# A graph attention kernel of two layers: prologue work regrouped and moved into the steps, one-hot products added in pairs

## Chip, cores and metric

The kernel runs on one core of one Trainium2 chip. The metric is the device time of one execution in microseconds (us). A core has a matrix engine (PE, with its weight loads shown as PEld), a vector engine (DVE), a scalar engine (ACT), a general engine (POOL) that also issues the indirect gathers, and a sync engine (SP) that issues plain transfers.

## The reference

A graph has N = 6250 nodes with 256 features and E = 200,000 edges with 32 attributes, sorted by destination. Rows of x are normalised and rectified, pass two graph attention layers (four heads of 64, then one of 256), and x is added at the end. Cut to what matters:

```python
def _gat(x, src, dst, ea, Wg, a_s, a_d, Wge, a_e, b, n, h, f):
    hx = (x @ Wg).reshape(n, h, f)
    he = (ea @ Wge).reshape(-1, h, f)
    al = leaky_relu(einsum(hx, a_s)[src] + einsum(hx, a_d)[dst] + einsum(he, a_e), 0.2)
    m = segment_max(al, dst)
    al = exp(al - m[dst]);  al = al / segment_sum(al, dst)[dst]
    out = segment_sum(hx[src] * al[:, :, None], dst)
    return out.reshape(n, h * f) + b

# te: edge attributes of a layer; a self loop with the mean of a node's te is added per node
te = relu(edge_attr @ We + be) * exp(x @ Wo + bo)[src][:, None]
h  = relu(layernorm(x))
x  = x + (_gat1(relu(_gat0(h) + h)) + relu(_gat0(h) + h) + h)
```

## The kernel before

**Tiles and steps.** The sorted edges are laid out as 128 partitions x 24 columns, a *step*. There are NS = 66 steps a layer (64 of 24 columns, then one of 14 and one of 13), numbered k = 0 to 131 over both layers. A table T of node rows (features after the weights, attention terms, an exponential) lies in memory for each layer; 24 indirect gathers of POOL (`gather`, L874) fetch the 128 source rows of each column into one of three buffers G.

**A step**, in the order in which its engines take the work: gathers of the next step; `logits` and `ends` (attention logits and two scans per edge row, with `pen`, a mask that is a large negative number where a destination begins); `spread` and `parts` of the next step (one-hots of destination blocks from `lb`, and parts of the node rows `tw`, which SP loads in `nodes`); `rphase1` of the next step (edge attributes times weights on PE, L958, rectified into R on ACT, L963); `links` (scans over 128 edge rows, L1096); `maxima`; `rphase2` and `adst` (into a PSUM tile `zad`, L972, L1032); `scale` (G times the weights, L1171); `sums` (one-hot products of G on PE, L1183), whose end frees G for the gathers of a later step; `edge_rows` (a transpose of zad, L1046); `onehots` (L1003); then the rows of the step before are finished and stored. `index_on` ends the step: seven turns of a generator that prepares the index masks of the next group of four steps (`index_group`). The order on each engine is the program's; waits are put in by the framework from tiles read and written.

**The prologue** (L201 to L401) makes T of layer 0. It loads x in 49 tiles (nine groups of two to seven) and gathers x for the 24 columns of step 0 (`first_rows`, L250; 8 gathers ahead of the loop, then one a tile from tile 4). These 24 columns are further tiles in G0, four groups of six. `stats` gives each group's mean and inverse root (DVE; for groups 3 to 8 a chain of small operations on POOL, L282 to L299); then each tile is normalised (ACT, L310), transposed (PE, L316; ACT, L318), multiplied (PE, L431) and kept with its bias (DVE, L435). A finished group is stored to T. `step(g)` hands out the turns of `stats` up to group g. Between the tiles DVE also takes the turns of `indices`, among them the checks of the index ranges (some 13 operations on one partition), and from the last tiles on those of `later`: folds of attention vectors into layer 0's edge weights and layer 1's weights (`fold`, `fold_e`, L170 to L195).

**Start of the steps.** `edges` (L616) zeroes five tiles `tws` on DVE (L633), loads and prepares step 0 and enters the loop.

**The layer boundary.** `ending` runs steps 64 and 65, whose node rows the first steps of layer 1 need, and prepares step 66, the first of layer 1. Step 66 gathers rows before the last 128 node rows are final, so `add_last` (L843) builds one-hots O from row numbers and adds 24 products with those 128 rows (`last`) into G, 260 columns wide:

```python
y = self.ps_y.tile([P, 1024], F32, name="y")
for i in range(c):
    h = y[:, 512 * (i % 2):512 * (i % 2) + L.TW]
    nc.tensor.matmul(h, st["O"][:, i, :], st["last"], start=True, stop=True)
    V.tensor_add(G[:, i, 0:L.TW], G[:, i, 0:L.TW], h)
```

`ps_y` and `ps_1` hold one buffer of each tile name (y, and zad, u).

Of the kernel before, what the change touches and what calls it, by code (L numbers as in the profile page):

```python
# [31 lines left out]
P = 128  # L32
# [47 lines left out]
class Kernel:  # L80
# [32 lines left out]
    def consts(self, wp):  # L113
# [3 lines left out]
        make_identity(nc, self.ident)  # L117
        self.wg, row, wpk = [], [], []
        self.ones = cp.tile([P, 1], F32, name="ones")
        nc.gpsimd.memset(self.ones, 1.0)  # L120
        self.bias, self.webd, self.be, wge = [], [], [], []
        for L in self.L:
            q = (nc.scalar, nc.sync)[L.l]
            wg = cp.tile([P, 2, L.MW], F32, name=f"wg{L.l}")
            q.dma_start(wg, a[f"wg{L.l}"].rearrange("(k p) m -> p k m", p=P))
            r = wp.tile([P, 3, D], F32, name=f"row{L.l}", bufs=1)
            q.dma_start(r.rearrange("p k d -> p (k d)"), a[f"row{L.l}"][0:3 * D].partition_broadcast(P))
            if L.l == 0:
                nc.scalar.activation(wp.tile([P, 1], F32, name="tab", bufs=1), self.ones, AF.Exp)
            self.wg.append(wg)  # L130
            row.append(r)
            b = cp.tile([P, L.MW], F32, name=f"bias{L.l}")
            nc.sync.dma_start(b, a[f"row{L.l}"][3 * D:].partition_broadcast(P))
            w = cp.tile([P, P + 1], F32, name=f"webd{L.l}")
            nc.sync.dma_start(w, a[f"we{L.l}"][:, 0:P + 1])
            e = wp.tile([P, D], F32, name=f"wge{L.l}", bufs=1)
            nc.sync.dma_start(e, a[f"we{L.l}"][:, P + 1:])
            self.bias.append(b)
            self.webd.append(w[:, 0:P])
            self.be.append(w[:, P:P + 1])  # L140
            wge.append(e)
# [29 lines left out]
        def fold(L):  # L171

            H = L.H
            for k in range(2):
                for j, c0 in ((0, L.p), (1, L.ad)):
                    t = wp.tile([P, D], F32, name="wtmp", bufs=4)
                    V.tensor_mul(t, self.wg[L.l][:, k, 0:D], row[L.l][:, j, :])
                    yield
                    V.tensor_reduce(self.wg[L.l][:, k, c0:c0 + H], t.rearrange("p (h f) -> p h f", h=H),
                                    axis=AX.X, op=OP.add)  # L180
                    yield

        def fold_e(L):

            H = L.H
            wea, we1 = self.wea[L.l]
            t = wp.tile([P, D], F32, name="wtmp", bufs=4)
            V.tensor_mul(t, wge[L.l], row[L.l][:, 2, :])
            yield
            V.tensor_reduce(we1, t.rearrange("p (h f) -> p h f", h=H), axis=AX.X, op=OP.add)  # L190
            yield
            for j in range(2):
                r = slice(j * PH, (j + 1) * PH)
                V.tensor_copy(wea[r, 32 * j:32 * j + H], we1[r, :])
            yield  # L195

        def later():
            yield from fold_e(self.L[0])
            yield from fold(self.L[1])
            yield from fold_e(self.L[1])  # L200

        return fold(self.L[0]), later()

    def prologue(self):
# [7 lines left out]
        with ExitStack() as c:  # L212
# [21 lines left out]
            warm = pt.tile([P, 2, P], F32, name="pT")  # L234
            for i in range(28):
                nc.tensor.matmul(warm[:, i % 2, :], self.ident, self.ident, start=True, stop=True)
# [18 lines left out]
            rows0 = first_rows()  # L255
            for _ in range(8):
                next(rows0, None)

            def stats(g):

                n, x = len(groups[g]), xs[g]
                st = wp.tile([P, GT, 6], F32, name="st", bufs=2)
                mv = wp.tile([P, GT, 2], F32, name="mv", bufs=3)
                s = wp.tile([P, 3, GT], F32, name="sc", bufs=3)
                for i in range(n):
# [35 lines left out]

            for i in range(0, CX, 6):
                xs[len(groups)] = G0[:, i:min(i + 6, CX), 0:D]
                groups.append(list(range(NT + i, NT + min(i + 6, CX))))
            tiles = [(g, i, t) for g, ts in enumerate(groups) for i, t in enumerate(ts)]
# [38 lines left out]
            def step(g):  # L344

                for q in list(ahead):
                    if q > g:
                        return
# [8 lines left out]
            for k in range(-3, len(tiles) + 1):  # L357
# [7 lines left out]
                if n0 is not None:  # L365
                    w = min(P, N + P - n0)
                    nc.sync.dma_start(self.T[1][n0:n0 + w, :], zero[:w, :2 * self.L[1].TW])
                    nc.sync.dma_start(self.part[n0:n0 + w, :], zero[:w, :self.L[1].TW])
                if 0 <= k + 1 < len(tiles):
                    turn(*tiles[k + 1])  # L370
# [12 lines left out]
                if t >= NT:  # L383
                    step(g + 2)
                if k >= 4:
                    next(rows0, None)
# [18 lines left out]
    def fixed_rows(self):  # L405
# [18 lines left out]
        for i in range(2):  # L424
            self.trow1.append(cp.tile([P, 2 * L1.TW], F32, name=f"t1row{i}"))
            nc.gpsimd.memset(self.trow1[i][:, L1.TW + D:], 0.0)

    def node_rows(self, L, hT, ps):
# [8 lines left out]
    def indices(self, wp):  # L437
# [74 lines left out]

        chk = wp.tile([1, 9, NS + 1], F32, name="chk", bufs=1)
        V.memset(chk, 0.0)
        V.tensor_scalar(chk[:, 0, :NS], ll[0:1, :], float(M - 1), None, op0=OP.is_gt)
        V.tensor_sub(qd[0:1], qlast[0:1], qbase[0:1])
        V.tensor_scalar(chk[:, 5:9, :NS], qd[0:1], 31.0, None, op0=OP.is_gt)
        nb = wp.tile([1, NS + 1], F32, name="nb", bufs=1)
        V.tensor_copy(nb[:, :NS], base[0:1, :])
# [5 lines left out]
        yield  # L525
        V.tensor_tensor(chk[:, 3, :NS], sc0[0:1, 0, :], sc0[0:1, 2, :], op=OP.is_lt)
        V.tensor_scalar(chk[:, 0, NS:], base[0:1, NS - 2:NS - 1], float(N - P), None, op0=OP.is_lt)
# [4 lines left out]
        yield  # L532
        self.before = cp.tile([P, NS], F32, name="before")
        V.tensor_copy(self.before, dpv)
        yield

    def index_tiles(self):
# [3 lines left out]
        for s in range(NS):  # L541
# [3 lines left out]
            else:  # L545
# [3 lines left out]
                                                    for n in ("loc", "fpen", "lpen", "isl"))  # L549
        self.pen = cp.tile([P, 4 * NCH + 1], BF, name="pen")  # L550
        self.bad = cp.tile([P, 1 + len(self.groups)], F32, name="bad")
# [11 lines left out]
    def index_group(self, g, pool, di):  # L563
# [23 lines left out]
        for pen, e in zip((self.fpen, self.lpen), ends):  # L587
# [5 lines left out]
            yield  # L593
        pv = self.pen[:, 4 * o:4 * (o + w)].rearrange("p (s h c) -> p s h c", h=4, c=c)
        t = pool.tile([P, 4 * C], F32, name="gt", bufs=2)
# [3 lines left out]
        yield  # L599
        V.tensor_scalar(pv[:, :, 0, :], t3, 1.0, -BIG, op0=OP.min, op1=OP.mult)  # L600
        V.memset(self.pen[:, 4 * (o + w):4 * (o + w) + 1], -BIG)
        yield
        for h in range(1, 4):
            nc.scalar.activation(pv[:, :, h, :], pv[:, :, 0, :], AF.Copy)
            yield
        t = pool.tile([P, 4 * C], F32, name="gt", bufs=2)
# [10 lines left out]
    def edges(self, ctx):  # L617
# [12 lines left out]
        self.state = {0: None, 1: None}  # L630
        self.tws = [self.np_.tile([P, self.L[0].TW + D], F32, name=f"tw{i}", bufs=1) for i in range(5)]
        for t in self.tws:
            nc.vector.memset(t, 0.0)  # L633
        self.nodes(steps[0])
# [9 lines left out]
        self.adst(steps[0])  # L644
        self.onehots(steps[0])
        self.edge_rows(steps[0])

        pv = late = None
        self.ahead, self.rest = 1, None
        for k, st in enumerate(steps):  # L650
# [45 lines left out]
            if pv:  # L696
                self.rows1(pv)
                late = pv
            self.index_on(left)
            if k + 6 == self.NS:  # L700
                self.places(steps[self.NS])
# [140 lines left out]
    def add_last(self, st):  # L842
# [4 lines left out]
                        op0=OP.subtract, op1=OP.is_equal)  # L847
        y = self.ps_y.tile([P, 1024], F32, name="y")
        for i in range(c):
            h = y[:, 512 * (i % 2):512 * (i % 2) + L.TW]  # L850
            nc.tensor.matmul(h, st["O"][:, i, :], st["last"], start=True, stop=True)
            V.tensor_add(G[:, i, 0:L.TW], G[:, i, 0:L.TW], h)

# [79 lines left out]
    def nodes(self, st):  # L933
        nc, L, s = self.nc, st["L"], st["s"]
        r = self.row(0, s)
        tw = self.tws[st["k"] % 5]
        st["tw"], st["xw"] = tw[:, :L.TW], tw[:, L.TW:L.TW + D]
# [11 lines left out]
    def rphase1(self, st):  # L949
        nc, L = self.nc, st["L"]  # L950
        l, ea = L.l, st["ea"]
        st["R"] = R = self.wp.tile([P, 2, 32 * C], F32, name="R", bufs=1)
        c = st["C"]
        for i in range(2):
# [97 lines left out]
    def logits(self, st):  # L1052
# [14 lines left out]
        yield  # L1067
        n, p0 = H * c, 4 * o
        fb, w = self.fb[st["k"] % 2], c if H > 1 else 1
        x = c - 1 + 32 * w  # L1070
        st["f"], st["b"] = f, b = fb[:, :n], fb[:, x:x + n]
        st["ends"] = fb[:, c - 1:c + (31 + H) * w:w]
        V.tensor_tensor_scan(f, self.pen[:, p0:p0 + n], al[:, :n], -BIG, op0=OP.add, op1=OP.max)
        yield
        V.tensor_tensor_scan(b[:, ::-1], self.pen[:, p0 + 1:p0 + n + 1][:, ::-1], al[:, :n][:, ::-1], -BIG,
                             op0=OP.add, op1=OP.max)
# [468 lines left out]
```

## Time and profile before

| | |
|---|---|
| runs, median (lowest to highest) | 4817.07 us (4813.92 to 4823.6) |
| profiled execution, its own time | 4800.02 us |
| its span | 4798.2 us |
| mean granted clock of PE over the span | 0.732 |
| prologue, until DVE begins with the steps | 0 to 145.9 us |
| layer 0, first gather to last burst before the boundary | 96.0 to 2437 us |
| boundary, three bursts and their waits | 2437 to 2624 us |
| layer 1, steady steps | 34.2 us each |

The profile lists groups of instructions by source line: busy time, then how long the engine was idle just before them and what released it. A line of the timeline has start, duration, engine, line, operation, output <- inputs, shape, and in brackets the idle time of that engine before it with the releaser. "issue" is idle time in which the engine waited for nothing that the profile shows; "remote" stands where the profile names no instruction of this core as releaser. How full the engines were in four stretches, from the view of windows (columns: stretch, its length, then busy time and number of instructions of PE, PEld, DVE, ACT and POOL, the granted clock, the share of the transfer engines and GB/s):

```profile
0.00:96.00 96.00, 78.48 (x382) 62.28 (x383) 69.93 (x319) 51.19 (x132) 48.42 (x145) 0.91 0.73 247
96.00:146.00 50.00, 27.44 (x114) 20.80 (x112) 21.66 (x97) 16.12 (x42) 22.90 (x24) 0.73 0.24 66
1000.00:1034.00 34.00, 25.82 (x80) 15.35 (x79) 23.25 (x53) 3.63 (x8) 22.84 (x25) 0.75 0.42 115
2537.00:2600.00 63.00, 29.64 (x48) 12.05 (x48) 10.68 (x26) 0.00 (x0) 39.17 (x41) 0.50 0.33 90
```

### The profile page before, as it was taken

Reading aid. Unit: us, or ns where it says so; the run is one execution under the profiler, and the core shown is the slowest. Engines: PE = TensorE matmul, PEld = TensorE weight load, DVE = VectorE, ACT = ScalarE, POOL = GpSimd, SP = SyncE. Lnnn points to the kernel's source line nnn. Section 1 sums busy time; section 2 is a strip of 40 time slices with the busy share of each in tenths; the row PEclk is TensorE's granted clock in tenths of the full one; section 3 lists DMA queues with packets and bytes.
Section 4 is the critical chain, followed back from the end, with each engine's and each line's share of the span. In section 5 each row is a group of like instructions: output and inputs, shape, how many; then the busy total and the mean of one; then the engine's idle time right before and its main releaser. Section 6 shows DMA issues by size and latency. Waiting matters only on the chain. (4 is left out here: it accounts for less than half of the span.)

```text
span 4798.2 us, 35104 instructions
## 1 busy us (share of the span) xinstructions
PE 3203.7 (67%) x9964; PEld 1948.6 (41%) x9964; DVE 2901.0 (60%) x6782; ACT 520.2 (11%) x1152; POOL 3011.0 (63%) x3249
## 2 busy tenths in 40 slices
PE   7556766767767766767765666666666666666666
PEld 5334444444444444444442333333333433333334
DVE  6556766666766666666664555555455556455556
ACT  4111111111111111111110000000000000000000
POOL 5446666666666666666644666666666666666664
PEclk8676777776777777777775777777767777777777
DMA  6334444444444444444433444444444444444442
GB/s 218 93 104 119 128 130 119 129 131 119 130 127 122 128 128 126 124 126 127 126 108 92 126 118 117 124 120 124 116 124 126 118 116 125 119 124 117 124 125 69
DMA packets 240006, 585.82 MB, mean 122 GB/s; under 512 B 64201, under 2 KB 96655, under 8 KB 239609
## 3 DMA queue, kind: packets, MB, share of 16 engines
q0 software_dynamic: 150144, 422.75, 33.6%
q1 hardware_dynamic: 89243, 160.09, 10.2%
q8 instruction: 80, 1.31, 0.1%
q14 instruction: 123, 1.01, 0.1%
q10 hardware_dynamic: 416, 0.67, 0.0%
HBM read 544.42 MB, written 38.94 MB: 122 GB/s over the span
## 5 line engine op out<-in xcount | busy, mean ns | idle before, releaser
L874 POOL DMA_INDIRECT G<-T,src x3078 | 2937.8, 954 | 1679.3 <-issue 889.1
L1183 PE MATMUL u<-G,S 128*128 128x270 f32 (+1 forms) x6252 | 1648.0, 417 | 737.7 <-issue 588.3
L1183 PEld LDWEIGHTS u<-G,S 128*128 128x128 f32 x6252 | 1257.7, 203 | 1066.7 <-issue 643.0
L958 PE MATMUL y<-ea,webd 64*128 64x384 f32 (+1 forms) x1056 | 709.6, 795 | 326.8 <-issue 293.1
L1171 DVE TENSOR_TENSOR G<-G,kps 128x6144 f32<-128x6144 f32 (+1 forms) x137 | 853.0, 6230 | 0.0
L1096 DVE TENSOR_TENSOR_SCAN cl<-fl,cl,lf 4x129 f32<-4x129 f32 (+1 forms) x130 | 61.1, 470 | 898.5 <-remote 598.6
L958 PEld LDWEIGHTS y<-ea,webd 64*128 64x128 f32 x1056 | 281.4, 289 | 605.0 <-issue 540.2
L972 PE MATMUL zad<-R,wea 128*64 128x384 f32 (+1 forms) x1056 | 447.3, 764 | 10.2 <-ACT R L963 7.3
L1003 DVE TENSOR_TENSOR S<-kps,loc 128x3072 f32<-128x3072 f32 x132 | 437.5, 3315 | 4.5
L963 ACT ACTIVATE R<-y,webd 128x768 f32<-128x768 f32 x260 | 233.2, 897 | 649.8 <-PE y L958 293.8
L972 PEld LDWEIGHTS zad<-R,wea 128*64 128x64 f32 x1056 | 149.8, 197 | 309.5 <-issue 246.9
L1188 ACT ACTIVATE U<-u 128x270 f32<-128x270 f32 (+1 forms) x132 | 52.0, 394 | 1852.8 <-remote 1004.5
L1046 DVE STREAM_TRANSPOSE rt<-zad 128x768 f32<-128x768 f32 (+1 forms) x130 | 124.6, 959 | 15.9 <-issue 10.7
L1018 PE MATMUL zad<-a,Q 128*128 128x12 bf16 (+1 forms) x132 | 23.9, 181 | 163.4 <-issue 99.6
L431 PE MATMUL fin<-wg,h1T 128*128 128x260 f32 x264 | 119.5, 599 | 1.5 <-ACT h1T L1278 1.5
L987 DVE TENSOR_TENSOR lb<-lb,kps 128x1536 bf16<-128x1536 bf16 (+1 forms) x68 | 113.5, 1669 | 0.0
L1086 PE MATMUL lf<-ident,fb 128*36 128x128 f32 (+1 forms) x132 | 45.8, 347 | 98.6 <-issue 69.2
L431 PE MATMUL ps<-wg,hT 128*128 128x266 f32 x292 | 88.3, 429 | 28.4 <-ACT hT L318 17.8
L1103 PE MATMUL lf<-ident,cl 36*128 36x36 f32 (+1 forms) x132 | 35.4, 269 | 95.9 <-DVE cl L1098 95.8
L1270 DVE TENSOR_TENSOR t1row<-t1row,fb 128x256 f32<-128x256 f32 x66 | 28.2, 427 | 112.5 <-remote 60.4
L1103 PEld LDWEIGHTS lf<-ident,cl 36*128 36x128 f32 (+1 forms) x132 | 25.3, 192 | 168.9 <-DVE cl L1098 148.7
L1018 PEld LDWEIGHTS <-Q 128*128 128x128 bf16 x132 | 14.3, 108 | 190.7 <-issue 108.1
(202 smaller groups left out, 2248.4 us busy)
## 6 DMA issues: line engine op xcount, KB each, us to landing
G<-T,src POOLq DMA_INDIRECT x3078
ea<-in_ea_dram SPq DMA_DIRECT2D x64, 768.0 KB
lb<-locrow SPq DMA_DIRECT2D x64, 384.0 KB
T<-t1row SPq DMA_DIRECT2D x66, 227.5 KB
tw<-T SPq DMA_DIRECT2D x66, 225.8 KB
tw<-T SPq DMA_DIRECT2D x66, 117.2 KB
tw<-in_x_dram SPq DMA_DIRECT2D x66, 112.0 KB
part<-t1row SPq DMA_DIRECT2D x64, 113.8 KB
```

What stands on the lines that cost most here:

```text
L431: self.nc.tensor.matmul(ps[:, :L.MW], hT[:, k, :], self.wg[L.l][:, k, :], start=(k == 0), stop=(k == 1))
L874: nc.gpsimd.indirect_dma_start(out=G[:, c, 0:L.TW], out_offset=None, in_=rows, in_offset=bass.IndirectOffsetOnAxis(ap=idx[:, c:c + 1], axi ...
L958: nc.tensor.matmul(y[:, o], self.webd[l][r, :], ea[r, w], start=True, stop=True)
L963: nc.scalar.activation(R[:, i, :32 * c].rearrange("p (b n) -> p b n", b=2), y.rearrange("p (b n) -> p b n", b=2)[:, :, :16 * c], AF.Relu, ...
L972: nc.tensor.matmul(st["zad"][i * PH:(i + 1) * PH, o], self.wea[l][0], R[:, i, w], start=True, stop=False)
L987: V.tensor_tensor(lb[:, :, :n], lb[:, :, :n], self.k_part.unsqueeze(2).to_broadcast([P, i, n]), op=OP.is_equal)
L1003: nc.vector.tensor_tensor(st["S"][:, c0:c1, :], self.k_iota.unsqueeze(1).to_broadcast(w), self.loc[:, o + c0:o + c1].unsqueeze(2).to_broad ...
L1046: V.transpose(rv[:, :32 * c].rearrange("p (b n) -> p b n", b=2), z.rearrange("p (b n) -> p b n", b=2)[:, :, :16 * c])
L1096: V.tensor_tensor_scan(cl[:H, :], fl[:H, :], lf[:H, 0:P + 1], init, op0=OP.add, op1=OP.max)
L1103: nc.tensor.transpose(pc, cl[:n, 0:P], self.ident[0:n, 0:n])
L1171: nc.vector.tensor_tensor(v, v, pw[:, c0:c1, :].unsqueeze(3) .to_broadcast([P, c1 - c0, H, L.F]), op=OP.mult)
L1183: nc.tensor.matmul(st["u"][:, :L.W], S[:, i, :], G[:, i, 0:L.W], start=(j == 0), stop=(j == c - 1))
```

## The change

1. **Gathers of x**: 14 instead of 8 ahead of the loop, the other ten at every third tile from tile 15 on instead of one a tile from tile 4.
2. **Statistics of step 0's columns** in groups of 6 and 18 instead of four of 6; turns for the group of 18 are handed out from tile 45 on only.
3. **tws**: four tiles instead of five, zeroed by POOL after the 14 gathers instead of by DVE at the start of `edges`; steps take them in turn modulo four.
4. **Moved out of the prologue**: layer 1's `fold` goes behind step 0's one-hots in `edges`; the checks and layer 1's `fold_e` are taken in two turns a step from k = 6 on. Their tiles move to the pool that stays.
5. **pen**: kept once per edge instead of four times (once a head); each step of layer 0 copies it fourfold on ACT at the start of `rphase1`, into one of two tiles `pen4`. `index_group` has 13 turns instead of 16.
6. **Idle products on PE**: 34 instead of 28 at the start, 8 more at tile 1 and 3 at tile 6.
7. **add_last**: products in pairs, into two PSUM tiles in turn (y and zad), and one add of two columns (128 x 520) for each pair.

```diff
-            for i in range(28):
+            def idle(n):
+                for _ in range(n):
+                    nc.tensor.matmul(self.kps[:, 384:512], self.ident, self.ident, start=True, stop=True)
+
+            for i in range(34):
                 nc.tensor.matmul(warm[:, i % 2, :], self.ident, self.ident, start=True, stop=True)
...
-            for _ in range(8):
+            for _ in range(14):
                 next(rows0, None)
+            for t in self.tws:
+                nc.gpsimd.memset(t, 0.0)
...
-            for i in range(0, CX, 6):
-                xs[len(groups)] = G0[:, i:min(i + 6, CX), 0:D]
-                groups.append(list(range(NT + i, NT + min(i + 6, CX))))
+            for i, e in ((0, min(6, CX)), (6, CX)):
+                if i < e:
+                    xs[len(groups)] = G0[:, i:e, 0:D]
+                    groups.append(list(range(NT + i, NT + e)))
...
-                    if q > g:
+                    if q > (g if k >= NT - 4 else min(g, g0)):
                         return
...
+                if k in (1, 6):
+                    idle(9 - k)
...
-                if k >= 4:
+                if k >= 14 and k % 3 == 0:
                     next(rows0, None)
...
-        def later():
-            yield from fold_e(self.L[0])
-            yield from fold(self.L[1])
-            yield from fold_e(self.L[1])
-
-        return fold(self.L[0]), later()
+        self.late, self.soon = fold_e(self.L[1]), fold(self.L[1])
+        return fold(self.L[0]), fold_e(self.L[0])
...
+        self.late = chain(self.late, self.checks(qd31, low))
...
-        self.pen = cp.tile([P, 4 * NCH + 1], BF, name="pen")
+        self.pen = cp.tile([P, NCH + 1], BF, name="pen")
+        self.nc.gpsimd.memset(self.pen[:, NCH:], -BIG)
+        self.pen4 = [cp.tile([P, 4 * C + 1], BF, name=f"pen4{i}") for i in range(2)]
...
-        V.tensor_scalar(pv[:, :, 0, :], t3, 1.0, -BIG, op0=OP.min, op1=OP.mult)
-        V.memset(self.pen[:, 4 * (o + w):4 * (o + w) + 1], -BIG)
-        yield
-        for h in range(1, 4):
-            nc.scalar.activation(pv[:, :, h, :], pv[:, :, 0, :], AF.Copy)
-            yield
+        V.tensor_scalar(self.pen[:, o:o + w], t[:, :w], 1.0, -BIG, op0=OP.min, op1=OP.mult)
+        yield
...
-        self.tws = [self.np_.tile([P, self.L[0].TW + D], F32, name=f"tw{i}", bufs=1) for i in range(5)]
-        for t in self.tws:
-            nc.vector.memset(t, 0.0)
...
         self.onehots(steps[0])
+        drain(self.soon)
         self.edge_rows(steps[0])
...
             self.index_on(left)
+            if k >= 6:
+                next(self.late, None)
+                next(self.late, None)
...
-        y = self.ps_y.tile([P, 1024], F32, name="y")
-        for i in range(c):
-            h = y[:, 512 * (i % 2):512 * (i % 2) + L.TW]
-            nc.tensor.matmul(h, st["O"][:, i, :], st["last"], start=True, stop=True)
-            V.tensor_add(G[:, i, 0:L.TW], G[:, i, 0:L.TW], h)
+        for i in range(0, c, 2):
+            y = self.ps_y.tile([P, 1024], F32, name="y") if i % 4 else self.ps_1.tile([P, 1024], F32, name="zad")
+            n = min(2, c - i)
+            h = y.rearrange("p (j w) -> p j w", j=2)[:, :n, :L.TW]
+            for j in range(n):
+                nc.tensor.matmul(h[:, j, :], st["O"][:, i + j, :], st["last"], start=True, stop=True)
+            g = G[:, i:i + n, 0:L.TW]
+            V.tensor_add(g, g, h)
...
-        tw = self.tws[st["k"] % 5]
+        tw = self.tws[st["k"] % 4]
...
-        c = st["C"]
+        c, o, H = st["C"], st["o"], L.H
+        st["pen"] = self.pen[:, o:o + c + 1]
+        if H > 1:
+            st["pen"] = pen = self.pen4[st["k"] % 2]
+            nc.scalar.activation(pen[:, :H * c].rearrange("p (h c) -> p h c", c=c),
+                                 self.pen[:, o:o + c].unsqueeze(1).to_broadcast([P, H, c]), AF.Copy)
```

## Prediction

> **What bounds the kernel now.** I read the engine totals first, then the costliest groups, the waits by releaser, and the timeline at four places: the prologue, the first steps, one steady step, the layer boundary. The page says which engine carries the steps:
>
> ```profile
> PE 3203.7 (67%) x9964; PEld 1948.6 (41%) x9964; DVE 2901.0 (60%) x6782; ACT 520.2 (11%) x1152; POOL 3011.0 (63%) x3249
> L874 POOL DMA_INDIRECT G<-T,src x3078 | 2937.8, 954 | 1679.3 <-issue 889.1
> L1188 ACT ACTIVATE U<-u 128x270 f32<-128x270 f32 (+1 forms) x132 | 52.0, 394 | 1852.8 <-remote 1004.5
> ```
>
> PE shows more busy time, but POOL sets the pace: one gather of a step is 0.95 us and the next starts 0.30 later, so 24 of them are a burst of 30 us, and the starts of the bursts lie 34.2 us apart in layer 1 and about 36 in layer 0. Between bursts POOL waits 4 to 6 us for the sums that free its buffer. The 1004.5 us that ACT waits with the releaser "remote" are one more trait: in a long part of each burst, until some 2 to 4 us after its last gather, the recorded semaphore updates of all engines land only about 0.7 us apart (110.89, 111.58, 112.28, 113.0, ... in step 1), so handing work from one engine to another is slow there. I call this a slow stretch. About 54 updates fall in a burst of layer 0 and 42 in one of layer 1. What the change can win lies where POOL isn't busy already. Those places are these:
>
> ```profile
> 46.14 0.43 DVE L435 TENSOR_TENSOR trow<-ps,bias 128x266 f32<-128x266 f32 x1 [3.10 <-PE pT L316]
> 49.60 0.60 ACT L310 ACTIVATE h<-x,ln 128x256 f32<-128x256 f32 x1 [2.20 <-POOL ln L299]
> 60.86 0.60 ACT L310 ACTIVATE h<-x,ln 128x256 f32<-128x256 f32 x1 [3.41 <-DMA part<-zero]
> 96.03 1.07 POOL L874 DMA_INDIRECT G<-T,src  x1 [18.40 <-ACT hT L318]
> 129.16 0.39 ACT L318 ACTIVATE hT<-pT 128x256 f32<-128x256 f32 x1 [13.83 <-remote]
> 146.05 0.95 POOL L874 DMA_INDIRECT G<-T,src  x1 [20.10 <-ACT G L329]
> 146.31 2.71 DVE L633 MEMSET tw<- 128x524 f32 x5 [0.38 <-issue]
> 162.65 0.98 DVE L1046 STREAM_TRANSPOSE rt<-zad 128x768 f32<-128x768 f32 x1 [7.05 <-issue]
> ```
> ```profile
> 2537.48 1.24 PE L851 MATMUL y<-last,S 128*128 128x260 f32 x2 [6.75 <-DVE S L846]
> 2538.76 0.43 DVE L852 TENSOR_TENSOR G<-G,y 128x260 f32<-128x260 f32 x1 [1.33 <-PE y L851]
> 2539.24 1.24 PE L851 MATMUL y<-last,S 128*128 128x260 f32 x2 [0.52 <-DVE G L852]
> ...
> 2575.36 0.42 DVE L852 TENSOR_TENSOR G<-G,y 128x260 f32<-128x260 f32 x1 [5.18 <-remote]
> ...
> 2599.51 0.43 DVE L852 TENSOR_TENSOR G<-G,y 128x260 f32<-128x260 f32 x1 [1.33 <-PE y L851]
> ...
> 2623.89 0.95 POOL L874 DMA_INDIRECT G<-T,src  x1 [35.52 <-PE zad L1018]
> ```
>
> The last fence matters most. For the first full step of layer 1, 24 one-hot products are added into the gathered rows. Both halves lie in one PSUM tile, so PE waits for DVE (0.52) and DVE for PE (1.33): 1.75 us a round, and 3.3 to 5.6 us for the seven rounds in a slow stretch (2563 to 2592). They end at 2599.94, the step's own chain ends 24 us later, and POOL, whose burst ended at 2588.4, has stood still for 35.52 us.
>
> **Part 1: the pairs (L846 to L852).** Removed: 12 adds of 0.43 us and all turns but those between tiles. With two tiles, PE fills one while DVE empties the other. A product costs PE 0.53 us by the warm L431 rows (1.06 for two such products) and 1.24 by the row above; 12 pairs are 13 to 30 us, against 62.5. An add of 128x520 is not in the trace; between 0.43 (this width halved) and 0.98 (128x768 transposed) I take 0.7, hidden behind the next pair. So the adds end between 2551 and 2568, before most of the slow stretch. But the next thing is POOL: its gathers go on to 2588.4 whatever PE does, and 4.3 us of a usual wait give 2592.7 as its earliest restart. The chain of 24 us after the adds now falls into the slow stretch; its six turns between PE and DVE cost up to 2.6 us each there (half of a 5.2 us round) instead of 1, so it ends between 2575 and 2602. Against 2623.89 that is a gain of 22 to 31; I take **28**, and for the range 15, if the stretch lasts longer.
>
> The windows give 0.50 as PE's granted clock from 2537 to 2600. The Trainium skill, TensorE: Matmul & The Clock Gate, section "Part 1: The HAM clock gate", says that the clock is halved until PE was active for about 3.4 us. By that rule the closer spaced pairs would soon be warm, and 12 pairs would take some 16 us, an estimate from it and the rows; by the row's 1.24 they take 30.
>
> **Part 2: gathers and statistics of the prologue.** Before, 13 gathers already run without a gap (5.67 to 22.0), though eight are issued ahead of the loop; so "fourteen first" changes little. The others ran in a bunch of six at 37.6 to 45.0 and one of five at 49.7 to 56.3, and POOL's own Newton steps (0.20 to 0.27 us each, some 15 for a group of tiles) stood behind them: hence the three waits of 3.10, 2.20 and 3.41 us. One gather at every third tile delays a chain by 1.25 us, not by 7.5. The undisturbed pace is 1.12 us a tile. Of the 8.7 us of these waits I take back 5. DVE is full from 80 to 100 us (18.96 of 20); the checks leave there (3.5 us of 78.92 to 84.7), and two groups of statistics instead of four save two Newton chains of 14 small operations (some 0.15 us each, 4 us, half of it in this stretch). Of these 5.5 us I take 3, as the last tiles are also bound by PE and ACT. The first gather of step 1, which waits for the last store, comes **8** earlier (bounds 3 and 12: only one of the waits, or all). Behind it the last ten tiles crawl through a slow stretch (the wait of 13.83); fewer updates there give **2** (0 to 6).
>
> **Part 3: zeroing tw.** 2.71 us of DVE right after the prologue go. On POOL it falls into an idle of 10.83 us after the first gathers (22.03 to 32.86), where 128x536 took 0.56 us: four are 2.3 us, hidden. Without that cover they would delay POOL's first Newton chain by as much. Gain **2.6**. The layer 1 folds (eight operations of 0.42) go into the 7.05 us in which DVE waits for PE ahead of L1046: nothing, or up to 4 if that wait is shorter by then. With four tiles instead of five, SP issues the loads of a step's own rows some 6 to 8 us later and with it what stands behind on its queue (lb, gi, fl, ea); each is needed some 30 us later, so nothing.
>
> **Part 4: what the steps receive.** The checks and layer 1's edge weights, some 17 small operations, fall on k = 6 to 8, two generator turns a step. DVE is not full there, but each update in a burst takes its place in a row of 0.35 to 0.7 us: **+5** (0 to +12). Per four steps the index work loses three copies on ACT and one memset, and each step gets one copy of `pen` on ACT ahead of R. The copies of before took 0.27 us (128x96), and ACT waits before R anyway:
>
> ```profile
> 1014.19 0.90 ACT L963 ACTIVATE R<-y,webd 128x768 f32<-128x768 f32 x1 [2.84 <-PE lf L1103]
> ```
>
> That 2.84 us is the cover; without it 65 steps would pay 0.27 each, 18 us. The number of instructions per step hardly changes. **0** (5 either way). The idle matmuls (6 and 11 more, 0.3 us each) fall where PE waits (2.52 us at 15.79, 3.18 at 24.69); at a clock of 0.50 the L431 group takes 2.14 us there, against 1.06 later at 1.00. If they raise the clock, up to four tiles gain 1.1 us each, and if they only stand in the way they cost 3; I take 0.
>
> **The sum.** 28 + 8 + 2 + 2.6 - 5 = 35.6 us less. The profiled execution took 4800.02 (span 4798.2), so 4764 for its like. The runs shown have a median of 4817.07, 17.05 above it, and I forecast on their level: **4781 us**. All best ends give 57 less, all worst ends nothing.
>
> **The rivals.**
> *The boundary gives it back (0.15).* The slow stretch ends with the burst, and a chain of many turns in it may end no sooner than some 15 us before the old time. For it: rounds grew there from 1.75 to 5.6. Against: the steady steps run the same chain inside a burst in 34.2 us. Then 4817 - 13 - 7.6 = 4796.
> *The pairs stay in step (0.1).* If the waits are counted so that PE still waits for the last add of the other tile, a pair costs 2.5 + 0.7 + two turns of 0.9 (the 1.33 and 0.52 less what they overlap), near 5 us in place of 3.5 for two rounds outside the stretch, but 12 rounds for 24 inside it: about 45 instead of 62. Gain 17 in place of 28: 4792.
> *The statistics bunch up (0.1).* 18 of them at 0.42 us stand behind the permission at k = 45 and are drained at once at k = 52; if this delays the last stores, the 8 of part 2 are lost: 4789.
> *The copy of pen shows (0.13), the slower side.* It stands on ACT ahead of R, in order, and with R the second layer of matmuls, adst and the transpose wait. If its wait or update takes a place in the row of updates in every layer 0 step, the step grows by up to 0.7, and by a second place 1.4. It breaks even with the rest at 35.6/64 = 0.56 us a step; at 1 us, 4781 + 64 = 4845, at 0.7 4826. For it: layer 0 steps are 36 us against 34.2, longer with more updates in a burst (54 against 42). Against: ACT's idle before R, and the three copies that go.
>
> **The numbers.** My forecast has 0.52, the rivals 0.48 together. 0.2% of 4817 is 9.6 us, about what runs of this kernel can tell from no change. Faster than 4807.4 are the forecast and most of the first three rivals; within it some of the first and the fourth's mild end; slower most of the fourth: 0.76, 0.12, 0.12. The forecast's own range is 4760 to 4803; with the rivals 4755 to 4815.
>
> **What would show it.** The pairs: 12 rounds from about 2530 (7.6 earlier), done in 13 to 30 us, and a POOL wait below 13 us where it was 35.52. The prologue: no ACT wait over 2 us at the places of 49.60 and 60.86, the first L874 gather near 88. Steps 6 to 8 up to 5 us longer in all; other layer 0 steps unchanged to 0.2 us. Wrong I am if layer 0 steps lengthen by half a microsecond, or if the wait at the boundary stays above 20.

## The result, and the profile after

The changed kernel takes 4781.99 us (median of 6 runs, 4764.79 to 4785.57) against 4820.31 us before (6 runs, 4813.92 to 4825.21): a ratio of 0.9914, 95% interval 0.9903 to 0.9925. The forecast was 4781 us. The size is right; most of the steps that made it are not, and the experiments are about that. Executions of one kernel differ by up to 25 us here, and a trace shows one of them.

First the page of the changed kernel: totals of the engines, and the groups of the gathers and of ACT's copy of the sums (L893 is the old L874, L1215 the old L1188).

```profile
PE 3213.8 (67%) x9998; PEld 1955.4 (41%) x9998; DVE 2894.3 (61%) x6722; ACT 523.8 (11%) x1162; POOL 3007.3 (63%) x3256
...
L893 POOL DMA_INDIRECT G<-T,src x3078 | 2931.5, 952 | 1660.2 <-issue 905.5
...
L1215 ACT ACTIVATE U<-u 128x270 f32<-128x270 f32 (+1 forms) x132 | 51.8, 393 | 1800.8 <-remote 791.1
```

Busy time is what it was; POOL's idle time ahead of gathers fell by 19.1 us (1679.3 to 1660.2), nearly the difference of the two spans (4798.2 to 4778.7). So the traces show 19.5 us of the 38: the profiled execution of before (4800.02) was 20 us under the median of the six runs, the one after 1.5 us. Where the 19.5 us lie, by the starts of the bursts of gathers (worked out from the timelines of POOL):

| start of the gathers of | before | after | difference |
|---|---|---|---|
| step 1 | 96.0 | 95.8 | -0.2 |
| step 6 | 332.0 | 316.3 | -15.7 |
| step 31 | 1225.1 | 1213.5 | -11.6 |
| step 67 | 2527.4 | 2515.8 | -11.6 |
| step 69 | 2623.9 | 2603.3 | -20.6 |
| step 131 (last) | 4735.3 | 4716.5 | -18.8 |

The prologue gave nothing, the boundary 9 us, the early steps 15.7 (5.4 of it from step 2's gathers to step 3's, 8.4 from step 4's to step 5's), and steps 6 to 31 gave back 4.1. The timeline of the changed kernel at the prologue, then two rows of before beside it, then the changed kernel at the boundary:

```profile
25.68 0.38 ACT L323 ACTIVATE hT<-pT 128x256 f32<-128x256 f32 x1 [13.94 <-remote]
82.11 8.34 SPq L340 DMA_DIRECT2D T<-trow  x3
96.39 0.60 ACT L315 ACTIVATE h<-G,ln 128x256 f32<-128x256 f32 x1 [4.12 <-DVE ln L300]
95.81 0.94 POOL L893 DMA_INDIRECT G<-T,src  x1 [12.84 <-issue]
146.72 0.94 POOL L893 DMA_INDIRECT G<-T,src  x1 [21.18 <-ACT G L334]
```
```profile
11.67 0.38 ACT L318 ACTIVATE hT<-pT 128x256 f32<-128x256 f32 x1
83.96 9.05 SPq L335 DMA_DIRECT2D T<-trow  x3
```
```profile
2525.98 2.07 PE L869 MATMUL zad<-last,S 128*128 128x260 f32 x4 [6.75 <-issue]
...
2531.31 1.05 PE L869 MATMUL y<-last,S 128*128 128x260 f32 x4
...
2532.40 0.70 DVE L871 TENSOR_TENSOR G<-G,y 128x520 f32<-128x520 f32 x1 [0.18 <-PE y L869]
2533.46 0.70 DVE L871 TENSOR_TENSOR G<-G,zad 128x520 f32<-128x520 f32 x1 [0.36 <-issue]
...
2541.51 0.70 DVE L871 TENSOR_TENSOR G<-G,y 128x520 f32<-128x520 f32 x1 [3.52 <-remote]
2547.11 0.70 DVE L871 TENSOR_TENSOR G<-G,zad 128x520 f32<-128x520 f32 x1 [4.90 <-remote]
2555.52 0.70 DVE L871 TENSOR_TENSOR G<-G,y 128x520 f32<-128x520 f32 x1 [7.72 <-remote]
2566.02 0.70 DVE L871 TENSOR_TENSOR G<-G,zad 128x520 f32<-128x520 f32 x1 [9.80 <-DMA G<-T,src]
2577.22 0.70 DVE L871 TENSOR_TENSOR G<-G,y 128x520 f32<-128x520 f32 x1 [10.50 <-remote]
...
2603.29 0.94 POOL L893 DMA_INDIRECT G<-T,src  x1 [26.62 <-PE zad L1044]
```

At the prologue a new wait stands at the very start: ACT copies the first transposed tile at 25.68 us, where before it did so at 11.67. The sixth tile is kept at 37.8 us instead of 30.0. The loop then makes it up: the last of the 49 tiles is kept at 89.4 instead of 92.0, and SP has issued the last three stores to T by 90.45 instead of 93.01. What was won is lost behind that: the first gather of the table follows 5.4 us after the last store's issue, where before it followed after 3.0. The other traces agree: 3.0 us in all four with the old prologue, 3.9 to 6.1 in all ten with the new one. POOL's last gathers of x now run until 83.0, beside these stores, where before they ended at 56.3; that they delay the stores is likely but was not tested. ACT's wait of 4.12 us for the statistics of the group of 18 ends at 96.39, behind the first gather of the table, so it isn't what held that gather.

At the boundary the first pairs go as forecast: two columns in about 1.0 us, where single adds took 3.5. But the slow stretch now begins at 2537, not at 2563, and from 2541 on two columns take 5.6, 8.4, 10.5 and 11.2 us, in the end what two single adds took there before (2 x 5.6). It lasts until the gathers beside it end (2576.7). POOL's wait fell from 35.52 to 26.62 only.

### The profile page after: what moved, and what is told of

Read it like the earlier page. It is cut to its first block, busy times and chain, and to the rows that moved or that the text cites. A ratio compares the mean times of both kernels' runs of the same rounds, so it can differ in the third digit from the quotient of the medians.

```text
span 4778.7 us, 35236 instructions
## 1 busy us (share of the span) xinstructions
PE 3213.8 (67%) x9998; PEld 1955.4 (41%) x9998; DVE 2894.3 (61%) x6722; ACT 523.8 (11%) x1162; POOL 3007.3 (63%) x3256
## 5 line engine op out<-in xcount | busy, mean ns | idle before, releaser
L893 POOL DMA_INDIRECT G<-T,src x3078 | 2931.5, 952 | 1660.2 <-issue 905.5
L1215 ACT ACTIVATE U<-u 128x270 f32<-128x270 f32 (+1 forms) x132 | 51.8, 393 | 1800.8 <-remote 791.1
L1113 PEld LDWEIGHTS lf<-ident,fb 128*36 128x36 f32 (+1 forms) x132 | 16.5, 125 | 180.5 <-issue 133.2
L439 PEld LDWEIGHTS fin<-wg,h1T 128*128 128x128 f32 x264 | 68.3, 286 | 43.8 <-issue 30.5
```

The lines of the kernel that those rows point to most:

```text
L439: self.nc.tensor.matmul(ps[:, :L.MW], hT[:, k, :], self.wg[L.l][:, k, :], start=(k == 0), stop=(k == 1))
L893: nc.gpsimd.indirect_dma_start(out=G[:, c, 0:L.TW], out_offset=None, in_=rows, in_offset=bass.IndirectOffsetOnAxis(ap=idx[:, c:c + 1], axi ...
L1113: self.nc.tensor.transpose(self.lf[0:e.shape[1], 1:P + 1], e, self.ident)
```

## The experiments

Several chips ran them, and one condition has to be told first: the kernel before took 4061.5 us on the chip of the first four experiments and 4815 to 4890 us on the others. Each kernel is compared with the kernel before on its own chip.

**Each half alone.** The kernel before with the new `add_last`; and the changed kernel with the old one:

```diff
-        y = self.ps_y.tile([P, 1024], F32, name="y")
-        for i in range(c):
...
+        for i in range(0, c, 2):
+            y = self.ps_y.tile([P, 1024], F32, name="y") if i % 4 else self.ps_1.tile([P, 1024], F32, name="zad")
...
```

> The kernel before with the new add_last alone (twelve pairs in two PSUM tiles), all else as before. In the two profiles the boundary (from the start of the burst of 48 gathers to the next burst) fell from 96.5 to 87.5 us, not by the 28 that I had forecast. Theory: that 9 us is what pairs are worth, because from the ninth pair on the adds go at 5.6 us a column, as single adds did: about 87 us here, and 9 us (0.998) off the time. Rival: the profile of before was taken in an execution 17 us under the median, and the boundary is worth more as a rule: 65 to 75 us at the boundary, 20 to 28 us off the time (0.995).

> The changed kernel with the old add_last (24 single adds into one PSUM tile), all else as changed. Theory: the prologue and the steps 1 to 4 hold the larger part, so the first gather of the table stays near 96 us, the burst of step 6 starts near 316 us (332 before), the boundary is 96 us again, and the time is about 29 us under that of before (0.994). Rival: pairs hold most of it, then about 10 to 15 us under before (0.997 or 0.998).

Pairs alone: 4045.95 us, 0.996 (0.9946 to 0.9974), 15.5 us less. All but the pairs: 4053.87, 0.9981 (0.9972 to 0.9991), 7.6 us less. Neither expectation was made for such a chip. The gathers' groups on the pages of pairs alone, and of a second trace of before on a chip like the first:

```profile
L877 POOL DMA_INDIRECT G<-T,src x3078 | 2935.5, 954 | 956.1 <-issue 903.3
```
```profile
L874 POOL DMA_INDIRECT G<-T,src x3078 | 2928.2, 951 | 1774.2 <-issue 898.6
```

The same 3078 gathers take 0.95 us each on both; but on the first chip POOL waits for next to nothing except the 0.30 us of issue between two gathers (903.3 of 956.1), on the other it waits 876 us besides the issue. Most of that is the 4 to 6 us behind each burst, and it is absent where no slow stretch is: bursts lie 30.1 us apart in layer 1, not 34 to 35. The pairs' boundary went there as I had argued: from step 67's first gather to step 69's 61.5 us with pairs, 73.8 without, and with pairs no wait is left.

**The idle products.** The changed kernel with 28 idle products at the start, none later:

```diff
-            for i in range(34):
+            for i in range(28):
...
-                if k in (1, 6):
-                    idle(9 - k)
```

> The changed kernel with 28 idle products at the start instead of 34 and none at tiles 1 and 6. In the changed profile ACT waits 13.94 us for the first transposed tile (11.7 to 25.7 us; 0 before) and eight idle products stand ahead of the next tile until 30.6. Theory: the updates of the added idle products queue ahead of the transposes' while the 14 gathers run, and the eight cost PE 2.6 us: without them the first tile is copied near 12 us, tile 6 is kept near 30 instead of 37.8, the first table gather comes at 88 to 91 and the time falls by 5 to 8 us against the changed kernel. Rival: the stall is that of an unbroken run of 14 gathers, whatever PE did: the wait stays at 13 us, and the time falls by 2 us or less.

4040.18 us, 0.9948 (0.9931 to 0.9964). The first table gather came at 84.1 us, with the products 83.2 and 86.1 in two other traces of this chip, and in none was the first tile late: undecided here, taken up again below.

**Holding the gathers.** Step 68's gathers wait for a mark behind the last add:

```diff
+        self.mark = self.cp.tile([1, 1], F32, name="mark")
+        V.memset(self.mark, 0.0)
...
+            if k == self.NS + 1:
+                m = self.cp.tile([1, 1], F32, name="mark2")
+                nc.gpsimd.tensor_copy(m, self.mark)
             self.gather(nx)
```

> The changed kernel with one tiny POOL copy ahead of the gathers of step 68 that waits for a mark which DVE writes behind the last add of add_last; so the 24 gathers of step 68 start only when the adds are done. Theory: the adds crawl because gathers run beside them. Once the 24 gathers of step 67 are through (30 us after the burst's start) the rest of the twelve pairs goes at 1.0 us each, step 68's gathers start near 33 to 36 us after the burst's start, and the boundary falls from 87.5 to 66 to 72 us: 15 to 21 us off the changed kernel's time. Rival: what crawls is DVE's wait for each column's own gather semaphore, whatever POOL does: the adds end no earlier than before (62 us after the burst's start), the held gathers end 30 us later and the boundary grows to 100 us or more, 12 us or more on the time.

4041.37 us, 0.9946 (0.9929 to 0.9963), 61.4 us at the boundary: nothing to hold for on that chip. It was run again below.

**Both kernels once more**, for second traces, on a chip with stretches.

> The kernel before, once more, for a second trace. In the first four experiments it took 4061.5 us, where the runs shown first have 4817, and no wait of POOL stood between its bursts (30.3 us from burst to burst). Theory: the slow stretches of the first trace are a state of the chip that a run finds and not a trait of the kernel; where they are missing the boundary interval before is the 61 us of 48 gathers and a wait of 10 to 15 us. Rival: the stretches are there in each run and only move: then the bursts would again lie 34 to 36 us apart and the time would be near 4800.

> The changed kernel, once more, beside the kernel before on the same chip. Theory: without slow stretches it gains what pairs alone gained (15.5 us) and what the rest alone gained (7.6 us), together 23 us or 0.9943; with slow stretches again 38 us or 0.992. Rival: the parts cover each other and only 16 us or 0.996 come.

Before: 4885.5 us in the execution of the trace, 4889.98 the median of seven others, with bursts 35 to 36 us apart, as the rival said. Changed: 4843.76, 0.9903 (0.9887 to 0.992), 46 us less. With 4061.5 us on another chip, the stretches go with the chip or with the time of the run; no run shows one chip both ways. The two traces put the difference elsewhere than the first pair: step 1 96.2 and 96.6, step 6 332.4 and 327.6, step 67 2558.0 and 2557.3, step 69 2654.8 and 2644.3, step 131 4821.1 and 4788.2. The boundary is 9.8 us again, steps 6 to 31 give back 6.2, and 22 us come in layer 1, of whose steps I had said nothing: 35.15 us each before, 34.8 after. Step 4's interval (45.3 and 45.0) moved by chance in the first pair: over the ten traces of chips with stretches it is 44.6 to 46.0 in five and 33.9 to 36.5 in five, of both kernels' forms.

**One wait for all gathers.**

```diff
+        t = self.cp.tile([1, C], F32, name="touch")
+        V.tensor_copy(t[:, :c], G[0:1, 0:c, 0])
         for i in range(0, c, 2):
```

> The changed kernel with one small DVE copy ahead of the twelve adds that reads a value of each of the 24 gathered columns, so that it takes all the waits for gathers and the adds have none of their own. If the chip shows slow stretches: theory, the adds crawl because each update passes slowly, so they stay at 5.6 us a column and the time is that of the changed kernel within 3 us; rival, each wait on a gather's semaphore is what costs 5.6 us, then the twelve adds take 13 to 16 us and the boundary falls by 17 to 21 us. If the chip shows none: both say no change, within 2 us.

4836.51 us, 0.9892 (0.9876 to 0.9909). The interval from step 68's gathers to step 69's is 55.9 us, 55.6 in the changed kernel's trace of that chip: the adds' own waits for gathers are not what crawls. The rival falls. The 7 us less in the median lie within what step 4 alone moves (33.9 here, 45.0 there).

**Four groups of statistics again.**

```diff
-            for i, e in ((0, min(6, CX)), (6, CX)):
+            for i in range(0, CX, 6):
+                e = min(i + 6, CX)
...
-                    if q > (g if k >= NT - 4 else min(g, g0)):
+                    if q > g:
```

> The changed kernel with the statistics of step 0's columns in four groups of six again and the turns handed out by the old rule. In the changed profile ACT waits 4.12 us at 96.39 for the group of 18, drained at once. Theory: the group of 18 bunches 18 statistics ahead of a store-bound stretch and costs what its two saved Newton chains bring: the first gather of the table comes within 1.5 us of the changed kernel's, and the time is the same within 2 us. Rival: fewer Newton chains are worth the 3 us that I forecast: the first gather comes 3 us later than in the changed kernel.

4838.46 us, 0.9895 (0.9873 to 0.9916), first table gather at 95.8 us against 96.6, and 6.1 us behind the last store's issue: two groups instead of four neither save nor cost anything that can be measured.

**The hold, where there is something to hold for.**

> The same kernel as in the fourth experiment (step 68's gathers held until the adds are done), since that chip showed no slow stretches and so had nothing to hold for. Where the stretches are there: theory, the adds crawl only beside gathers; the pairs left over when step 67's gathers end go at 1.0 us each, and the interval from step 67's first gather to step 69's falls from 87 us (56 + 31) to 66 to 72, 15 to 21 us off the changed kernel's time. Rival: the adds crawl on without gathers, the held ones end later and the interval grows to 100 us or more. On a chip without stretches: 61 us, no change.

4823.67 us against 4888.95, 0.9868 (0.9851 to 0.9884). The interval from step 67's gathers to step 69's is 74.2 us (39.0 and 35.2) instead of 87.0. The timeline where step 67's gathers end:

```profile
2583.16 0.95 POOL L898 DMA_INDIRECT G<-T,src  x1 [0.30 <-issue]
2586.14 0.70 DVE L874 TENSOR_TENSOR G<-G,zad 128x520 f32<-128x520 f32 x1 [6.34 <-remote]
...
2587.57 0.70 DVE L874 TENSOR_TENSOR G<-G,y 128x520 f32<-128x520 f32 x1 [0.73 <-remote]
...
2589.03 0.70 DVE L874 TENSOR_TENSOR G<-G,zad 128x520 f32<-128x520 f32 x1 [0.76 <-PE zad L872]
...
2591.55 0.19 POOL L681 COPY mark<-mark 1x1 f32<-1x1 f32 x1 [7.45 <-DVE mark L876]
2592.27 0.97 POOL L898 DMA_INDIRECT G<-T,src  x1 [0.53 <-issue]
```

The add at 2586.14 had waited 6.34 us beside gathers; 2 us after the last of them the next follow at 1.4 to 1.7 us. It is the gathers that slow the adds. The expected 15 to 21 us are 12.8, since the sixth to the ninth pair had met the stretch already.

**Four tw tiles alone.** The kernel before with four tiles in turn instead of five:

```diff
-        self.tws = [self.np_.tile([P, self.L[0].TW + D], F32, name=f"tw{i}", bufs=1) for i in range(5)]
+        self.tws = [self.np_.tile([P, self.L[0].TW + D], F32, name=f"tw{i}", bufs=1) for i in range(4)]
...
-        tw = self.tws[st["k"] % 5]
+        tw = self.tws[st["k"] % 4]
```

> The kernel before with four tw tiles in turn instead of five, all else as before. Theory: on a chip with slow stretches the changed kernel's 22 us in layer 1 (34.8 us a step against 35.15, in the traces of one chip) come from SP, which with four tiles waits for a tile and so issues the loads of tw some 10 to 16 us later in a step (18.8 us behind the burst's start instead of 3 to 9): 34.8 us a step here too, 20 us off the time of before. Rival: they come from another part or are chance: 35.15 a step and the time of before within 5 us. On a chip without stretches: no change, 30.1 us a step.

4856.16 us against 4888.95, 0.9943 (0.9927 to 0.996): 33 us less, the largest part of the change on such a chip. Layer 1's step is 34.75 us, against 35.15 in the second trace of before, which is of another chip with nearly the same time; that makes 24 us for its 60 full steps at 0.40. Step 4 took 36.4 in this trace, 9 less, which comes and goes by chance. The queue of SP in a step of layer 1 (window from the burst's first gather on), first in the second trace of before (burst at 3285.50), then with four tiles (burst at 3266.78):

```profile
3286.41 0.60 SPq L924 DMA_DIRECT2D fl<-flags  x2
3287.76 0.33 SPq L1324 DMA_DIRECT2D out_dram<-fb  x1
3288.59 0.34 SPq L939 DMA_DIRECT2D tw<-T  x1
```
```profile
3267.69 0.59 SPq L924 DMA_DIRECT2D fl<-flags  x2
3269.03 0.33 SPq L1324 DMA_DIRECT2D out_dram<-fb  x1
3285.61 0.33 SPq L939 DMA_DIRECT2D tw<-T  x1
```

In this step the load of tw leaves 3.1 us after the burst's start before, and 18.8 us after it with four tiles. Before, the loads go round in four steps: two in one step (near 9.9 and 20.5 us), none in the next, one near 9.5, one near 3.1. These steps take 35.8, 34.4, 35.0 and 35.5 us in that trace, so the one without a load is the shortest; with four tiles each step has one load near 18.8 and takes 34.6 to 34.9. But the first trace of before has its loads at much the same places (7.6 and 18.9, none, 7.6, 2.9), and its steps take 34.1 to 34.5, no longer than those of the changed kernel's first trace. That the rotation alone brings the gain on this chip is shown; by what path it shortens the step is not.

**A pause for POOL, and the hold with fewer idle products.** The hold with 16 tiny memsets between the 12th and 13th gather of a layer 1 step; and the hold with the edit of the third experiment:

```diff
+            if L.l and k > self.NS + 2 and j == 12:
+                for _ in range(16):
+                    nc.gpsimd.memset(self.rest_t, 0.0)
```

> The kernel of the hold with one more edit: from the third step of layer 1 on, POOL does 16 tiny memsets between the 12th and the 13th gather of a step, about 2 us in which it gathers nothing; layer 0 stays as it was and serves as the control. In the changed kernel's first trace step 4 took 36.5 us with a chance pause of 2.16 us in its burst, and 45.0 without one in the other. Theory: the other engines' updates pass while POOL pauses, so the 4.3 to 5 us that POOL waits after each burst of layer 1 shrink to 1 or 2 and a step takes 32.5 to 33.5 us where it took 34.8: 80 to 140 us off the time on a chip with slow stretches (and some 120 us more on one without). Rival: a pause only moves the waiting: 36 to 37 us a step in layer 1, 80 us more or beyond.

> The kernel of the hold with 28 idle products at the start and none at tiles 1 and 6. On the chips with slow stretches each trace of the changed kernel has the first transposed tile copied only near 25 us (11.7 in those of before) and the first table gather near 96 us, as before the change. Theory: the added idle products' updates stand ahead of the first transposes' in the stretch of the 14 gathers; without them the first tile is copied near 12, and the first table gather comes at 88 to 91, 5 to 8 us off the time of the hold. Rival: the unbroken 14 gathers and the memsets behind them alone hold the first tile back: 25 us and 96 us again, the same time within 2 us.

The pause: 4779.79 us, 0.9926 (0.991 to 0.9943); the other: 4759.81, 0.9892 (0.9875 to 0.9909), both against 4814.64. The memsets took 3.8 us of POOL's time, not 2, and the wait behind a burst shrank to 0.3 in three steps of four and to some 3 in the fourth, 1.1 on average where it was 4.5: a step of 34.49 us, against 34.25 without the pause on the same chip. Neither theory holds as a whole: the pause does let the others catch up, and it takes as long as the wait it replaces, so nothing is won. Whether a shorter one wins was not tried.

Fewer idle products: the first tile is copied at 21.43 us after a wait of 9.88 (25.63 and 13.91 in the trace with the pause, on the same chip), the first table gather comes at 93.0 instead of 96.7. So the added products are 4 us of the late start. The other 10 us are there without them; what holds them (the 14 gathers, or the memsets behind) was not separated.

## Why the prediction came out

The forecast of 36 us less (38 measured) was right, and so were its direction and its range; but the sum came out by luck. Its largest terms failed, and by its own sign it was wrong at the boundary, where the wait stayed above 20 us (26.62). On other chips an edit that I had costed at nothing made up for this. On the chip of the forecast the traces show 19.5 of the 38 us, 8.4 of them in step 4 by chance; where the rest lies no trace shows.

- **The pairs, 28: 9 to 10 measured on chips with stretches.** The forms were right: 0.70 us an add, 0.95 to 1.1 us a pair, no waiting in step. What failed is the step "the adds end between 2551 and 2568, before most of the slow stretch": the last add began at 2577.22, 49 us after the first, where I had 13 to 30 for all twelve rounds. I had taken the stretch as fixed in time, from 2563 to 2592. It goes with the gathers beside it, as the hold shows, and seemingly with the work done there: it came after six pairs, where before it came after 14 single columns, and stayed until the gathers ended. "Up to 2.6 us" for a turn in it was also too little; a pair, two turns, cost up to 11.2. (The rows of before have six rounds of 3.3 to 5.6 us, not seven; the next took 2.1.) So at this place the first rival (a gain of 13) was the better forecast. Where no stretch is, the argument held: no wait is left at the boundary, and the pairs bring 15.5 us. The Trainium skill, TensorE: Matmul & The Clock Gate, section "Part 1: The HAM clock gate", bears on the first pairs, with a clock that is halved until PE was active for about 3.4 us. The trace agrees in kind: 2.07 us for the pair at 2525.98, at a granted clock of 0.50, and 1.05 from 2531.31 on, 5.3 us later (3.6 in the second trace of the hold). In the stretch they are at 2.10 again.
- **The prologue, 8 and 2: nothing on chips with stretches,** 2.5 to 5.4 where there are none (first table gather at 88.6 us with the old prologue, 83.2 to 86.1 with the new). The waits at 49.60 and 60.86 did go, as I said they would. What I had missed is the start and the end. That "fourteen first" changes little, and the 0 for the idle products, failed, as the first tile then came 14 us late. Even so the last tile was kept 2.5 us earlier, and 5.0 to 7.3 where no stretches are; but I had taken the first gather to follow the last store as closely as before, and it follows 2.3 us later. The third rival saw the wait for the group of 18, 4.12 us; that wait cost nothing, since four groups bring the same.
- **tw zeroed by POOL, 2.6:** step 2's interval fell by some 5.2 (39.4 or 39.6 before, 34.1 to 34.4 in all seven traces with the edit); four tiles alone leave it at 39.5, so it is this edit, the folds' new place or another part of the change. Where no stretches are it is nothing (30.3 and 30.0 to 30.2).
- **Four tw tiles, 0: 33 alone on one chip, 24 of them in layer 1.** I had asked only whether a later load could come too late, found 30 us of slack, and wrote "so nothing". That the rotation could shorten the step was not among my cases. This is the largest error: 33 us, where the pairs and the prologue together lack 28.
- **Checks and edge weights in the steps, +5:** 2.1 and 2.7 in steps 6 to 8, where I had put them, and 4.1 and 6.2 from step 6 to step 31. That lies in my range. But from step 6 to step 31 four traces of two other chips give 907.7 to 920.7 us with these steps, and two give 902.3 and 904.7 without, so little more than the sign can be read.
- **pen, 0:** layer 0's steps took 35.85 us before and 35.86 after (mean of steps 11 to 60), 36.37 and 36.35 on the other chip. Right; the slower rival falls.

One thing stays open: the first pair of traces has 34.27 and 34.29 us a step in layer 1, so the rotation shows nothing there. That trace of before was 20 us under its median; whether its other executions had longer steps in layer 1 isn't in a trace.

The version that beats both kernels is the hold: 4823.67 us, 0.9868 of before, where the changed kernel had 0.9903 on a chip whose kernel before differed by 1 us; the two were not run on one chip with stretches. With fewer idle products it took 0.9892 on a third chip; the intervals overlap, so which of the two is better isn't decided.

## What to carry to other kernels

A slow place in a trace has a cause, not a time: before a piece of work is moved past it, ask what runs beside it, or one finds it again at the new place. An edit that makes a transfer wait is to be costed in both directions; here it brought 33 us, by a path that stays open. A stage that ends earlier helps only if what waits for it follows as closely as before. A sum that comes out right proves none of its terms; undoing one part at a time does.

## What the runs showed of the hardware

- The same kernel took 4061.5 us on one chip and 4815 to 4890 on the others, with gathers of 0.95 us on all. Nearly all of the difference is POOL's idle time ahead of gathers (956 and 1774 us on two pages). It goes with the slow stretches: there the other engines get their turns late while POOL gathers, and a step has 4 to 5 us in which POOL doesn't gather (4.5 behind a burst, or 3.8 in its middle and 1.1 behind it).
- In a stretch the starts of the adds lie a multiple of 0.70 us apart: 5.6, 8.4, 10.5 and 11.2 us, whatever the add itself takes (0.43 or 0.70). What is served in these 0.70 us isn't shown.
- The prediction read the slow stretch off the recorded semaphore updates, and these records are not complete there. By the program some 55 updates of the engines fall in a burst of layer 0; the first trace of before records 30 of them, the traces without stretches all. The starts of the adds are the better witness. No execution here is known to have run without the profiler, so a part of the recording itself in the stretches isn't excluded.
